# Row norms of an attention-like score matrix: scores with swapped operands, squares on ScalarE, the transpose by VectorE blocks and DMAs

## The chip, the cores and the metric

The kernel runs on one core of a Trainium2 chip. A core has TensorE (matrix products, with weight loads that overlap them), VectorE, ScalarE, GpSimd, and a queue on SyncE that starts most of its DMAs; the engines run side by side and wait for one another through semaphores. The metric is the device time in microseconds (us), from launch to the last result. Before the change it is 2290.54 us, the median of three runs (2290.47 to 2291.78).

## What is computed

The input x holds 128 matrices of 128 rows (nodes) and 512 columns, in float32; adj is one 128x128 matrix. Four layers follow one another, each with a residual and a layer norm over the 512 columns:

```python
# layer 0: x = layernorm(x + (adj @ x) @ W0 + bias0)
# layer 1: x = layernorm(x + L1(x)), the layer that the change touches:
    q = jnp.einsum('bnd,ed->bne', neuron_states, Wq)
    k = jnp.einsum('bnd,ed->bne', neuron_states, Wk)
    v = jnp.einsum('bnd,ed->bne', neuron_states, Wv)
    rel = jnp.einsum('bnd,bmd->bnm', q, k)
    rel = adjacency.T[None, :, :] * rel
    rel = rel / jnp.linalg.norm(rel, axis=2, keepdims=True)
    return jnp.einsum('bnm,bmd->bnd', rel, v)
# layer 2: graph attention (softmax over a masked leaky relu) and elu
# layer 3: relu of a row maximum of adj @ x, plus a bias, added to x
```

In layer 1, rel has a row for each query n and a column for each key m. Its rows are divided by their Euclidean norm, which is a sum over m, and the last product sums over m too.

## The kernel before

The 128 matrices go through in 32 groups of G = 4. Every step of every layer is a small function with a place in time (in slots of about 2.48 us); all of them are sorted by place, so that the layers of neighbouring groups interleave and each engine gets its instructions in that order. Group g's places are 28 slots after those of group g - 1. The names below are the ones that the profile shows; P = 128, K = 4 blocks of the 512 columns, D = 512.

```python
TABLE = dict(
    load=[-20], y=row(0.5, 1), ..., y_w=row(7, 1, 7), ...
    turn=row(21.4, 1), x_sums=row(25.3, 0.5), m=row(28, 1, 7), scores=row(36.5, 1),
    masked=[39.95], norms=[42.5], inverse=[43.1], v=row(42, 1, 7), attend=row(50.6, 1),
    residual=row(51.0, 1), ...
    turn_att=[68.6], with_beta=[69.0], gather=row(71.5, 1), ...
    widen=[98.7, 100.0, 103.6, 104.6], ..., store=[108.5],
)
# the last groups have places of their own (LAST)
```

Layer 1 does not form q and k. It forms xT (x turned, a tile of 512 columns on 4 blocks), then tT, the product of xT with the joined weight m_qk = Wq^T Wk, turned as well. From these two come the scores. Before, they are formed with the key m on the partitions and the query n along the free axis, which is the way round that the last product needs for its stationary operand (a TensorE product sums over partitions: out = lhsT^T rhs):

```python
def scores(b):
    if b == 0:
        s["p"] = bank(f"p_rel_{g}")
    for k in range(K):
        pe.matmul(
            s["p"][:, b * P : (b + 1) * P],
            s["xT"][:, k, b * P : (b + 1) * P],
            s["tT"][:, k, b * P : (b + 1) * P],
            start=(k == 0),
            stop=(k == K - 1),
        )

def masked():
    s["rel"] = work.tile([P, G, P], FP, tag="rel", name=f"rel_{g}", bufs=2)
    dve.tensor_tensor(
        s["rel"], s["p"].rearrange("p (b n) -> p b n", b=G), adj_b, ALU.mult
    )
    s["sq"] = work.tile([P, G, P], FP, tag="sq", name=f"sq_{g}")
    pool.tensor_tensor(s["sq"], s["rel"], s["rel"], ALU.mult)
```

The squared norm of a query is then a sum over partitions. TensorE makes it, as a product of the squares with a column of ones:

```python
def norms():
    p = bank(f"p_n_{g}")
    for b in range(G):
        pe.matmul(p[:, b : b + 1], s["sq"][:, b, :], ones, start=True, stop=True)
    s["p"] = p

def inverse():
    n2 = small.tile([P, G], FP, tag="n2", name=f"n2_{g}")
    dve.tensor_copy(n2, s["p"][:, :G])
    s["rn"] = small.tile([P, G], FP, tag="rn", name=f"rn_{g}")
    pool.tensor_tensor(s["rn"], n2, mhalf, ALU.pow)

def attend(b):
    s["o", b] = bank(f"p_o1_{g}_{b}")
    pe.matmul(s["o", b], s["rel"][:, b, :], s["v"][:, b, :], start=True, stop=True)
```

The division by the norm comes after that product, in the residual on VectorE (x2 = o * rn + x1). The weighted products m, v, y_w and z_w are seven block products each, three PSUM buffers at a time; their results are copied by ScalarE (fresh blocks) or added by VectorE:

```python
ORDER = (1, 2, 6, 5, 7, 3, 4)
REGION = {1: 0, 6: 0, 7: 0, 4: 0, 2: 1, 5: 2, 3: 2}
...
    def out(i):
        p, dst = r[REGION[i]], c(*BLOCK[i])
        if fresh and i in (1, 6, 5, 4):
            act.copy(dst, p)
        else:
            dve.tensor_tensor(dst, p, dst, ALU.add)
```

In the profile r_y, r_m, r_v and r_z are these products, p_rel the scores, p_n the norms, p_o the product with v, p_a, p_z, p_xT, p_eT and p_s products of the other layers.

Of the kernel before, what the change touches and what calls it, by code (L numbers as in the profile page):

```python
# [8 lines left out]
FP = mybir.dt.float32  # L9
AF = mybir.ActivationFunctionType  # L10
# [19 lines left out]
def kernel(  # L30
# [31 lines left out]

    nc = tc.nc
    pe, dve, act, pool = (InOrder(tc, e) for e in (nc.tensor, nc.vector, nc.scalar, nc.gpsimd))
    B, N, D = x.shape
    P = 128
    assert N == P and D % P == 0
    K = D // P
    H = D // 2
    G = 4  # L70
    NG = B // G
# [8 lines left out]
    def bank(name):  # L80
        return psum.tile([P, D], FP, tag="ps", name=name)
# [10 lines left out]
    def load(g):  # L92
        x1[g] = data.tile([P, G, D], FP, tag="x1", name=f"x1_{g}", bufs=3)
        if g == 0:
            for b in range(G):
                nc.sync.dma_start(x1[g][:, b, :], x[b])
        else:
            nc.sync.dma_start(x1[g], x[g * G : (g + 1) * G].rearrange("b n d -> n b d"))

    load(0)  # L100
    w0_sb = const.tile([P, K, D], FP)
# [19 lines left out]

    ident = const.tile([P, P], FP)
    make_identity(nc, ident)
    ones = const.tile([P, 1], FP)
    dve.memset(ones, 1.0)
    mhalf = const.tile([P, G], FP)
    dve.memset(mhalf, -0.5)

# [2 lines left out]
    pe.transpose(pt[:, :P], adj_sb, ident)  # L131
    act.copy(adjT, pt[:, :P])
    adj_b = adj_sb[:, None, :].to_broadcast([P, G, P])

    m_qk = const.tile([P, K, D], FP)
    wvT = const.tile([P, K, D], FP)
# [82 lines left out]
    def emit(at, f, *args):  # L219
        pieces.append((at, lambda: f(*args)))  # L220

    def each(at, f):
        for b in range(len(at)):
            emit(at[b], f, b)

    def row(at, step, n=G):
        return [at + i * step for i in range(n)]
# [3 lines left out]
        load=[-20], y=row(0.5, 1), bias=row(1.3, 1), y_sums=row(5.2, 0.5), y_w=row(7, 1, 7),  # L231
        stats0=row(14.4, 0.4), norm0=[16.2], apply0=row(16.8, 0.33),
        turn=row(21.4, 1), x_sums=row(25.3, 0.5), m=row(28, 1, 7), scores=row(36.5, 1),
        masked=[39.95], norms=[42.5], inverse=[43.1], v=row(42, 1, 7), attend=row(50.6, 1),
        residual=row(51.0, 1), dots=row(54.2, 1.1), norm1=[55.2], scale=[58.8],
        apply1=row(65.4, 0.33),
        spread=[61.6], leaky=[62.0], weighted=[63.4], greatest=[64.3], exps=[64.4],
# [23 lines left out]
        ),  # L261
        NG - 1: dict(
            m=[0.0, 1.73, 3.46, 5.2, 7.4, 9.1, 10.8], scores=row(12.7, 0.9), masked=[16.4],
            norms=[20.2], inverse=[21.1], v=[16.7, 18.4, 21.0, 22.7, 25.3, 27.9, 30.5],
            attend=row(33.2, 0.86), residual=row(34.1, 1.65), norm1=[40.65], dots=row(40.7, 1.53),
            scale=[47.0], apply1=row(47.5, 0.8), spread=[48.9], leaky=[49.4], weighted=[51.0],
            greatest=[52.4], exps=row(53.2, 0.6), divide=row(53.9, 0.6),
# [170 lines left out]
    def layer1(g, t):  # L438
        s = {}

        def turn(b):
            if b == 0:
                s["xT"] = work.tile([P, K, G * P], FP, tag="aT_x", name=f"xT_{g}")
            p = bank(f"p_xT_{g}_{b}")
            for k in range(K):
                pe.transpose(
                    p[:, k * P : (k + 1) * P], x1[g][:, b, k * P : (k + 1) * P], ident
                )
            act.copy(
                s["xT"][:, :, b * P : (b + 1) * P], p.rearrange("p (k n) -> p k n", k=K)  # L450
            )

        def begin_middle():
            s["tT"] = work.tile([P, K, G * P], FP, tag="nat", name=f"tT_{g}", bufs=3)

        def begin_values():
            s["v"] = work.tile([P, G, D], FP, tag="nat", name=f"v_{g}", bufs=3)

        def middle_block(nh, ch):
            return s["tT"][:, 2 * ch : 2 * ch + 2, 2 * P * nh : 2 * P * (nh + 1)]  # L460

# [3 lines that stand above are left out]
            for k in range(K):  # L465
                pe.matmul(
                    s["p"][:, b * P : (b + 1) * P],
                    s["xT"][:, k, b * P : (b + 1) * P],
                    s["tT"][:, k, b * P : (b + 1) * P],
                    start=(k == 0),  # L470
                    stop=(k == K - 1),
                )

        def masked():
            s["rel"] = work.tile([P, G, P], FP, tag="rel", name=f"rel_{g}", bufs=2)
            dve.tensor_tensor(
                s["rel"], s["p"].rearrange("p (b n) -> p b n", b=G), adj_b, ALU.mult
            )
            s["sq"] = work.tile([P, G, P], FP, tag="sq", name=f"sq_{g}")
            pool.tensor_tensor(s["sq"], s["rel"], s["rel"], ALU.mult)  # L480

        def norms():
            p = bank(f"p_n_{g}")
            for b in range(G):
                pe.matmul(p[:, b : b + 1], s["sq"][:, b, :], ones, start=True, stop=True)
            s["p"] = p

        def inverse():
            n2 = small.tile([P, G], FP, tag="n2", name=f"n2_{g}")
            dve.tensor_copy(n2, s["p"][:, :G])  # L490
            s["rn"] = small.tile([P, G], FP, tag="rn", name=f"rn_{g}")
            pool.tensor_tensor(s["rn"], n2, mhalf, ALU.pow)

        def attend(b):
            s["o", b] = bank(f"p_o1_{g}_{b}")
            pe.matmul(s["o", b], s["rel"][:, b, :], s["v"][:, b, :], start=True, stop=True)

        def residual(b):
            if b == 0:
                x2[g] = data.tile([P, G, D], FP, tag="x2", name=f"x2_{g}")  # L500
            dve.scalar_tensor_tensor(
                x2[g][:, b, :],
                s["o", b],
                s["rn"][:, b : b + 1],
                x1[g][:, b, :],
                op0=ALU.mult,
                op1=ALU.add,
            )
            stats(s, f"1_{g}", b, x2[g][:, b, :])


        def dots(b):
            if b == 0:
                s["d"] = small.tile([P, 2, G], FP, tag="d12", name=f"d12_{g}")
            for i in range(2):
                scr = work.tile([P, D], FP, tag="scr", name=f"scr_{g}_{b}_{i}", bufs=2)
                dve.scalar_tensor_tensor(
                    scr,
                    x2[g][:, b, :],
                    1.0,  # L520
                    wa[:, i, :],
                    op0=ALU.mult,
                    op1=ALU.mult,
                    accum_out=s["d"][:, i, b : b + 1],
                )

        def scale_dots():
            for i in range(2):
                dve.scalar_tensor_tensor(
                    s["d"][:, i, :],  # L530
                    s["mv"][:, :, 0],
                    wa_sum[:, i : i + 1],
                    s["d"][:, i, :],
                    op0=ALU.mult,
                    op1=ALU.add,
                )
            dve.tensor_tensor(
                s["d"], s["d"], s["r", 0][:, None, :].to_broadcast([P, 2, G]), ALU.mult
            )
            s12[g] = s["d"]  # L540

        each(t["turn"], turn)
        left_factors(t["x_sums"], s, "xT", "s_x", f"x_{g}", 1)
        product(t["m"], f"m_{g}", by_columns, s, "m", middle_block, True, begin_middle)
        each(t["scores"], scores)
        emit(t["masked"][0], masked)
        emit(t["norms"][0], norms)
        emit(t["inverse"][0], inverse)
        product(t["v"], f"v_{g}", by_rows, s, "v", rows_of(lambda: s["v"]), True, begin_values)
        each(t["attend"], attend)  # L550
        each(t["residual"], residual)
        each(t["dots"], dots)
        emit(t["scale"][0], scale_dots)
        norm(t["norm1"], t["apply1"], s, f"1_{g}", lambda: x2[g])
# [139 lines left out]
    def layer3(g, t):  # L694
        s = {}

        def widen(b):
            s["a", b] = bank(f"p_a_{g}_{b}")
            pe.matmul(s["a", b], adjT, x3[g][:, b, :], start=True, stop=True)

        def top(b):
            x = x3[g][:, b, :]
            mx = small.tile([P, 1], FP, tag="mx", name=f"mx_{g}_{b}")
            dve.tensor_reduce(mx, s["a", b], AX.X, ALU.max)
            tp = small.tile([P, 1], FP, tag="top", name=f"top_{g}_{b}")
            dve.tensor_scalar(tp, mx, b3_sb, 0.0, op0=ALU.add, op1=ALU.max)
            act.activation(x, x, AF.Identity, bias=tp)

        def store(i):
            for b in range(i * n, i * n + n):  # L710
                nc.sync.dma_start(out[g * G + b], x3[g][:, b, :])

        n = G // len(t["store"])
        each(t["widen"], widen)
        each(t["top"], top)
        each(t["stats3"], lambda b: stats(s, f"3_{g}", b, x3[g][:, b, :]))
        norm(t["norm3"], t["apply3"], s, f"3_{g}", lambda: x3[g])
        each(t["store"], store)
# [42 lines left out]
```

## Time and profile before

| engine | busy us | share of the span of 2288.5 us |
|---|---|---|
| TensorE, matrix products | 2250.7 | 98% |
| TensorE, weight loads | 1914.8 | 84% |
| VectorE | 1577.0 | 69% |
| ScalarE | 1005.3 | 44% |
| GpSimd | 959.2 | 42% |

| group of instructions (whole run) | count | mean ns of one |
|---|---|---|
| TensorE p_n<-ones,sq, one column | 256 | 240 |
| TensorE weight load of p_n | 256 | 192 |
| TensorE weight load of p_o | 256 | 191 |
| VectorE rel<-p_rel,adj_sb, 128x512 | 32 | 680 |
| VectorE copy n<-p_n, 128x4 | 32 | 151 |
| VectorE e<-e,rs, 128x128 | 4 | 293 |
| GpSimd sq<-rel, 128x512 | 32 | 1051 |
| ScalarE Exp, 128x128 | 128 | 390 |
| ScalarE read of the accumulator after it | 128 | 187 |
| ScalarE table load | 1 | 1283 |

A product of float32 stands as two records, with a weight load before each. Ends of matmul records are modelled, and neighbours overlap; starts are better to reckon with. The 16 DMA engines are busy a tenth of the time or so after the start; the queue's hardware moved 70.86 MB in 37,536 packets, in 8.7% of 16 engines' span.

### The profile page before, as it was taken

What the parts mean: (1) busy time and instruction counts of PE and PEld (TensorE: products, weight loads), DVE (VectorE), ACT (ScalarE), POOL (GpSimd) and SP (SyncE); (2) the same over time, 40 slices, a digit from 0 to 9 for tenths busy, and PEclk for the clock granted to TensorE, in tenths of its full rate; (3) what the DMA queues carried; (4) which work ended last, traced back from release to release, by engine and by line L of the source; (5) the groups of instructions that cost most, each with busy time, mean ns of one, the idle gap of its engine ahead of it and who ended that gap; (6) DMA issues with size and microseconds to landing.
All of it is one profiled execution on the core that took longest, in us unless ns stands there. A gap on an engine that the chain in (4) does not pass through costs nothing.

```text
span 2288.5 us, 31182 instructions
## 1 busy us (share of the span) xinstructions
PE 2250.7 (98%) x11809; PEld 1914.8 (84%) x11809; DVE 1577.0 (69%) x3319; ACT 1005.3 (44%) x1800; POOL 959.2 (42%) x775
## 2 busy tenths in 40 slices
PE   7999999999999999999999999999999999999996
PEld 5888888888888888888888888888888888888873
DVE  4656776666776667766667766667767677666677
ACT  2224444444444454444444444444444544444435
POOL 4434444344444334444344443444443344443422
PEclk9999999999999999999999999999999999999998
DMA  4000011100111100111100111001111001110001
GB/s 162 19 19 10 28 38 38 37 21 18 38 37 37 38 19 19 38 37 38 37 10 28 38 37 37 21 18 38 37 37 38 19 20 37 37 38 19 9 12 55
DMA packets 38886, 75.21 MB, mean 33 GB/s; under 512 B 3024, under 2 KB 3152, under 8 KB 38736
## 3 DMA queue, kind: packets, MB, share of 16 engines
q1 hardware_dynamic: 37536, 70.86, 8.7%
q10 hardware_dynamic: 1200, 2.36, 0.3%
q8 instruction: 93, 1.52, 0.3%
q14 instruction: 57, 0.47, 0.1%
HBM read 39.65 MB, written 33.55 MB: 32 GB/s over the span
## 4 chain that ended last, share of the span: by engine, by line
PE 94%; DVE 4%; POOL 1%; ACT 1%; issue 1%; DMA 0%; ACTq 0%; DVEq 0%; POOLq 0%
PE r_y L26 17%; PE r_v L26 16%; PE r_m L26 16%; PE r_z L26 16%; PE p_z L26 5%; PE p_rel L26 5%; PE p_o L26 5%; PE p_a L26 5%; PE p_y L26 5%; PE p_xT L26 2%; DVE x L26 1%; PE p_n L26 1%; DVE st L26 1%; PE p_eT L26 1%; PE p_m L26 1%; PE p_s L26 1%
## 5 line engine op out<-in xcount | busy, mean ns | idle before, releaser
L26 ACT ACTIVATE x<-x,nmean,rstd 128x512 f32<-128x512 f32 x512 | 386.4, 809 | 128.0 <-DVE nmean L26 127.9
L26 DVE BATCH_NORM_STATS2 st<-x 128x6 f32<-128x512 f32 x512 | 352.4, 688 | 75.3 <-ACT x L26 66.6
L26 POOL TENSOR_TENSOR rstd<-ve,mhalf 128x4 f32<-128x4 f32 (+1 forms) x134 | 144.5, 1078 | 245.3 <-DVE ve L26 241.3
L26 POOL TENSOR_TENSOR x<-x,bias_sb 128x512 f32<-128x512 f32 x128 | 174.8, 1368 | 145.5 <-PE p_y L26 145.5
L26 DVE SCALAR_TENSOR_TENSOR scr<-x,wa 128x512 f32<-128x512 f32 x256 | 214.9, 891 | 0.0
L26 ACT ACTIVATE x<-x,top 128x512 f32<-128x512 f32 x128 | 92.4, 722 | 254.1 <-DVE top L26 189.7
L26 DVE TENSOR_TENSOR x<-r_y,x 128x512 f32<-128x512 f32 x224 | 152.9, 683 | 54.4 <-PE r_y L26 44.5
L26 DVE TENSOR_TENSOR v<-r_v,v 128x512 f32<-128x512 f32 x96 | 65.8, 685 | 177.0 <-PE r_v L26 174.0
L26 POOL TENSOR_TENSOR s_x<-xT 128x512 f32<-128x512 f32 x64 | 82.2, 1285 | 222.2 <-ACT xT L26 222.2
L26 ACT COPY yT<-p_y 128x512 f32<-128x512 f32 x128 | 75.0, 586 | 206.0 <-PE p_y L26 206.0
L26 DVE SCALAR_TENSOR_TENSOR x<-p_o,rn,x 128x512 f32<-128x512 f32 x128 | 95.9, 749 | 99.5 <-PE p_o L26 96.5
L26 DVE SCALAR_TENSOR_TENSOR x<-m,x 128x512 f32<-128x512 f32 x128 | 115.1, 899 | 61.7 <-ACT m L26 51.3
L26 ACT COPY c<-r_z 128x512 f32<-128x512 f32 x124 | 72.6, 585 | 175.9 <-DVE scr L26 151.5
L26 PEld LDWEIGHTS p_y<-adjT,x 128*128 128x128 f32 x1024 | 135.3, 194 | 12.9 <-ACT adjT L26 5.0
L26 PEld LDWEIGHTS p_z<-eT,x 128*128 128x128 f32 x1024 | 135.4, 194 | 8.3 <-DVE x L26 1.2
L26 PE MATMUL p_y<-adjT,x 128*128 128x128 f32 x1024 | 136.1, 278 | 6.2 <-ACT adjT L26 4.7
L26 PEld LDWEIGHTS p_rel<-tT,xT 128*128 128x128 f32 x1024 | 134.2, 192 | 7.4 <-DVE tT L26 0.8
L26 PE MATMUL p_a<-x,adjT 128*128 128x512 f32 x256 | 133.6, 607 | 3.5 <-DVE mx L26 1.8
L26 PE MATMUL p_z<-eT,x 128*128 128x128 f32 x1024 | 136.4, 277 | 0.4 <-DVE x L26 0.4
L26 PE MATMUL p_rel<-tT,xT 128*128 128x128 f32 x1024 | 135.0, 275 | 0.6 <-DVE tT L26 0.6
L26 POOL TENSOR_TENSOR s_z<-zT 128x512 f32<-128x512 f32 x31 | 39.2, 1265 | 223.9 <-ACT zT L26 223.9
L26 PE MATMUL p_o<-v,rel 128*128 128x512 f32 x256 | 130.6, 594 | 0.0
(120 smaller groups left out, 5075.2 us busy)
## 6 DMA issues: line engine op xcount, KB each, us to landing
out_dram<-x SPq DMA_DIRECT2D x128, 256.0 KB, 2.0
x<-in_x_dram SPq DMA_DIRECT2D x31, 1024.0 KB, 5.2
w_sb<-in_L_gnn_weight_dram ACTq DMA_DIRECT2D x1, 1024.0 KB, 5.7
x<-in_x_dram SPq DMA_DIRECT2D x4, 256.0 KB, 7.5
wq_sb<-in_L_gnn_Wq_dram SPq DMA_DIRECT2D x1, 1024.0 KB, 11.7
wk_sb<-in_L_gnn_Wk_dram SPq DMA_DIRECT2D x1, 1024.0 KB, 14.6
w_sb<-in_L_gnn_W_dram ACTq DMA_DIRECT2D x1, 1024.0 KB, 10.2
wv_sb<-in_L_gnn_Wv_dram SPq DMA_DIRECT2D x1, 1024.0 KB, 13.7
```

Source lines behind the costliest of these rows:

```text
L26: return lambda *args, **kw: self.tc.keep_in_program_order(op(*args, **kw))
```

## The change

The scores are multiplied the other way round, so that the query n lies on the partitions. A row norm is then a sum along the free axis, and ScalarE can form it while it squares, by its accumulator: no product with ones and no copy out of PSUM. The product with v still needs the key m on the partitions, so rel has to be turned. VectorE turns it in blocks of 32x32 within their bands of 32 partitions, and sixteen DMAs per group carry the blocks from band to band, SBUF to SBUF. Two matrices of a pair are interleaved element by element, so that each run of a DMA is 64 elements (256 bytes) long; the product with v then reads its weights with a step of two elements. The purpose is to take the norm products off TensorE. The DMAs on SyncE's queue (loads, these moves, stores) are kept in program order.

```diff
+    sync = InOrder(tc, nc.sync)
+    Q = P // 32
-            nc.sync.dma_start(x1[g], x[g * G : (g + 1) * G].rearrange("b n d -> n b d"))
+            sync.dma_start(x1[g], x[g * G : (g + 1) * G].rearrange("b n d -> n b d"))
...
-    ones = const.tile([P, 1], FP)
-    dve.memset(ones, 1.0)
+    adjT_b = adjT[:, None, :].to_broadcast([P, G, P])
...
-        masked=[39.95], norms=[42.5], inverse=[43.1], v=row(42, 1, 7), attend=row(50.6, 1),
+        masked=[39.95], squares=[40.4], turn_rel=[40.3],
+        move_rel=row(41.2, 0.1), inverse=[42.5], v=row(42, 1, 7), attend=row(50.6, 1),
...  (the last group)
-            norms=[20.2], inverse=[21.1], v=[16.7, 18.4, 21.0, 22.7, 25.3, 27.9, 30.5],
+            squares=[17.2], turn_rel=[17.1], move_rel=row(18.0, 0.1), inverse=[20.0], v=[16.7, 18.4, 21.0, 22.7, 25.3, 27.9, 30.5],
...  (scores)
+                    s["tT"][:, k, b * P : (b + 1) * P],
                     s["xT"][:, k, b * P : (b + 1) * P],
-                    s["tT"][:, k, b * P : (b + 1) * P],
...  (masked)
-                s["rel"], s["p"].rearrange("p (b n) -> p b n", b=G), adj_b, ALU.mult
-            )
-            s["sq"] = work.tile([P, G, P], FP, tag="sq", name=f"sq_{g}")
-            pool.tensor_tensor(s["sq"], s["rel"], s["rel"], ALU.mult)
-
-        def norms():
-            p = bank(f"p_n_{g}")
+                s["rel"], s["p"].rearrange("p (b n) -> p b n", b=G), adjT_b, ALU.mult
+            )
+
+        def squares():
+            s["n2"] = small.tile([P, G], FP, tag="n2", name=f"n2_{g}")
             for b in range(G):
-                pe.matmul(p[:, b : b + 1], s["sq"][:, b, :], ones, start=True, stop=True)
-            s["p"] = p
+                scr = work.tile([P, P], FP, tag="sq", name=f"sq_{g}_{b}", bufs=2)
+                act.activation(
+                    scr, s["rel"][:, b, :], AF.Square, accum_out=s["n2"][:, b : b + 1]
+                )
+
+        def turn_rel():
+            s["relB"] = work.tile([P, 2, Q, 2 * P // Q], FP, tag="relB", name=f"relB_{g}")
+            s["relT"] = work.tile([P, 2, 2 * P], FP, tag="relT", name=f"relT_{g}")
+            for b in range(G):
+                dve.transpose(
+                    s["relB"][:, b // 2].rearrange("p q (u j) -> p q u j", j=2)[:, :, :, b % 2],
+                    s["rel"][:, b, :].rearrange("p (q u) -> p q u", q=Q),
+                )
+
+        def move_rel(a):
+            n = P // Q
+            for q in range(Q):
+                sync.dma_start(
+                    s["relT"][q * n : (q + 1) * n, :, 2 * a * n : 2 * (a + 1) * n],
+                    s["relB"][a * n : (a + 1) * n, :, q, :],
+                )
 
         def inverse():
-            n2 = small.tile([P, G], FP, tag="n2", name=f"n2_{g}")
-            dve.tensor_copy(n2, s["p"][:, :G])
             s["rn"] = small.tile([P, G], FP, tag="rn", name=f"rn_{g}")
-            pool.tensor_tensor(s["rn"], n2, mhalf, ALU.pow)
+            pool.tensor_tensor(s["rn"], s["n2"], mhalf, ALU.pow)
...  (attend)
-            pe.matmul(s["o", b], s["rel"][:, b, :], s["v"][:, b, :], start=True, stop=True)
+            pe.matmul(
+                s["o", b],
+                s["relT"][:, b // 2, :].rearrange("p (n j) -> p n j", j=2)[:, :, b % 2],
+                s["v"][:, b, :],
+                start=True,
+                stop=True,
+            )
...  (store)
-                nc.sync.dma_start(out[g * G + b], x3[g][:, b, :])
+                sync.dma_start(out[g * G + b], x3[g][:, b, :])
```

More of the change, by code (lines that the diff above doesn't have):

```diff
@@ L454, in begin_middle @@
             s["tT"] = work.tile([P, K, G * P], FP, tag="nat", name=f"tT_{g}", bufs=3)
-        def begin_values():
-            s["v"] = work.tile([P, G, D], FP, tag="nat", name=f"v_{g}", bufs=3)
         def middle_block(nh, ch):
@@ L494, in attend, with begin_values @@
+        def begin_values():
+            s["v"] = work.tile([P, G, D], FP, tag="nat", name=f"v_{g}", bufs=3)
         def attend(b):
             s["o", b] = bank(f"p_o1_{g}_{b}")
-            pe.matmul(s["o", b], s["rel"][:, b, :], s["v"][:, b, :], start=True, stop=True)
+            pe.matmul(
[5 more added lines that the diff above has]
+            )
@@ L546, in layer1 @@
         emit(t["masked"][0], masked)
-        emit(t["norms"][0], norms)
+        emit(t["squares"][0], squares)
+        emit(t["turn_rel"][0], turn_rel)
+        each(t["move_rel"], move_rel)
         emit(t["inverse"][0], inverse)
```

## The prediction

> **What bounds the kernel now.** I read the page's first part and its chain, then TensorE's waits, then one period of the trace, and last the groups that the change touches. First part and chain:
>
> ```profile
> PE 2250.7 (98%) x11809; PEld 1914.8 (84%) x11809; DVE 1577.0 (69%) x3319; ACT 1005.3 (44%) x1800; POOL 959.2 (42%) x775
> ...
> PE 94%; DVE 4%; POOL 1%; ACT 1%; issue 1%; DMA 0%; ACTq 0%; DVEq 0%; POOLq 0%
> ```
>
> TensorE is busy 98% of the span and carries 94% of the chain that ended last. Busy matmul rows overlap, so the share alone proves little. The stretches table for one group of four matrices in the steady part settles it:
>
> ```profile
> 1206.00:1275.46 69.46, 69.46 (x370) 59.61 (x369) 48.01 (x103) 31.27 (x56) 29.92 (x25) 1.00 0.09 31
> ```
>
> The columns are the stretch, its length, then the busy time of TensorE, its weight loads, VectorE, ScalarE and GpSimd. TensorE has no gap: the 69.46 us period is its instruction stream laid end to end. The list of TensorE's own waits adds up to about 25 us over the run, and each entry occurs once or twice, at the start or the tail; none recurs by group. So only two things can move the time: a shorter TensorE stream, or a new wait that TensorE sees.
>
> TensorE's timeline around the row norms; columns are start, length, engine, operation, tiles, count:
>
> ```profile
> 1242.57 1.89 PE L26 MATMUL r_v<-wvT,xT 128*128 128x256 f32 x8
> 1244.29 0.95 PE L26 MATMUL p_n<-ones,sq 128*128 128x1 f32 x8
> 1245.10 1.10 PE L26 MATMUL p_a<-x,adjT 128*128 128x512 f32 x2
> 1246.05 1.89 PE L26 MATMUL r_v<-wvT,xT 128*128 128x256 f32 x8
> 1247.77 1.05 PE L26 MATMUL p_z<-eT,x 128*128 128x128 f32 x8
> 1248.66 1.02 PE L26 MATMUL p_a<-x,adjT 128*128 128x512 f32 x2
> 1249.52 1.89 PE L26 MATMUL r_v<-t_v,s_x 128*128 128x256 f32 x8
> ```
>
> The ends of matmuls are modelled and overlap, so I use steps from start to start. From p_n to the next r_v is 1246.05 - 1244.29 = 1.76 us; the p_a within it costs 1249.52 - 1248.66 = 0.86 us where it stands alone. The four norm products therefore take 0.90 us of the period, though each makes one column: their eight weight loads are what is paid.
>
> Next the slack of the other engines at the same place. VectorE, then ScalarE, from the score product's mask on (the last column is idle time before, and its releaser):
>
> ```profile
> 1239.82 0.68 DVE L26 TENSOR_TENSOR rel<-p_rel,adj_sb 128x512 f32<-128x512 f32 x1
> 1240.60 0.69 DVE L26 TENSOR_TENSOR x<-r_y,x 128x512 f32<-128x512 f32 x1
> 1241.21 0.68 DVE L26 TENSOR_TENSOR eT<-p_eT,beta_i 128x512 f32<-128x512 f32 x1
> 1242.77 0.69 DVE L26 TENSOR_TENSOR x<-r_y,x 128x512 f32<-128x512 f32 x1 [0.88 <-PE r_y L26]
> ```
>
> ```profile
> 1239.33 2.93 ACT L26 ACTIVATE x<-x,nmean,rstd 128x512 f32<-128x512 f32 x4 [2.58 <-DVE nmean L26]
> 1244.49 0.59 ACT L26 COPY v<-r_v 128x512 f32<-128x512 f32 x1 [2.23 <-PE r_v L26]
> ```
>
> VectorE has an idle 0.88 us and ScalarE 2.23 us just where the new work goes in. The consumer of the turned matrix comes much later: the first p_o starts at 1266.88 us, 26 us after the mask.
>
> [...] No strided weight load is in this trace.
>
> **The change, part by part.**
>
> 1. Norm products leave TensorE: 32 groups x 0.90 us = -28.8 us, all on the path, since TensorE is never idle there. The last group's step is alike (2203.96 to 2204.87 us).
>
> 2. Scores with the operands swapped: the same 16 products, in 32 records per group of 128 columns over 128x128 weights. The step stays 0.88 to 0.89 us per matrix: 0.
>
> 3. GpSimd loses the squares (32 x 1.05 = 33.6 us), VectorE the copy of n (32 x 0.15 = 4.8 us). Neither engine bounds: 0.
>
> 4. ScalarE gets four Squares with accumulator per group. By the Exp row 390 ns and by the accumulator read 187 ns, 128 x 0.577 = 74 us of busy time; ScalarE goes from 44% to about 48%. The four Exps start every 0.39 us (1230.85, 1231.24, 1231.63, 1232.02), so four Squares fill 1.56 us. They begin when the four applies end, at 1242.26, and end near 1243.9, before the copy of v at 1244.49: hidden, 0. The inverse norms come earlier than before, because n waited for TensorE and VectorE until 1247.10.
>
> 5. VectorE gets four block transposes. [...] p_z wants eT only at 1247.77: 0.
>
> 6. Sixteen DMAs per group move rel between partitions. A store's issue takes 332 ns on the queue (its row) and lands after 2.0 us. 16 x 0.332 + 2.0 = 7.3 us after the transposes, near 1249 us. By bytes: 256 KB in 1024 pieces of 256 B; a packet of before took 8.7% x 16 x 2288.5 / 37,536 = 85 ns of one engine at mostly 2 KB, so at most 64 x 0.085 = 5.4 us on 16 engines. p_o is then due at 1266.0: about 16 us spare. In queue order the load of two groups later stands before them (1207.89, when 1 MB needs 5.2 us) and stores some 26 us after them, so neither is held up. 0.
>
> 7. p_o reads its weights at a step of two. [...]
>
> 8. The last group has less room. There ScalarE's Squares stand before the copy of v that started at 2201.95; they wait for rel until 2202.4, so that copy ends near 2204.6, while the third r_v step, which adds into the same bank, would now start at 2203.96: about +0.6 us. relT is whole near 2203.5 + 7.3 = 2210.8, p_o starts at 2217: 0.
>
> Sum: 2290.5 - 28.8 + 0.6 = 2262.3; with 0.7 us for small tail effects, **2263 us**, -1.2%. The period should go from 69.46 to 68.56 us.
>
> **Rivals.**
>
> A. The transfer becomes the wait. If each DMA had to follow the landing of the one before, 16 x 2.0 = 32 us would be needed where 25 are there: TensorE would stall some 7 us per group, 32 x 7 = 224 us, about 2490. Against it: four DMAs of before were issued within 2.18 us at the start, while each took 7.5 us to land, so they overlap. About 4%.
>
> B. TensorE pays for p_o. Weights at a step of two could load at half rate; the first load of three of the four p_o hides behind a transpose step of only 0.11 us, so it would add 3 x 0.1 us; and the first p_o now waits for many DMA semaphores, perhaps 0.2 us. 32 x 0.5 = 16 us, time 2279. For it: nothing in the trace excludes it. About 15%.
>
> C. VectorE or ScalarE slips into the path. If a transpose takes 0.6 us, the four take 2.4, the last x<-r_y slips by about 1.5 us and the bank that the second r_v needs comes late, by some 0.5 us per group: 2279 again. A table reload for Square between Exps, 1.28 us twice a group, would stay hidden in most groups. About 8%.
>
> D. The norm step's time is not given back, because something else sets the period. Against it: 69.46 of 69.46 us busy. 3%.
>
> **Range and chances.** The gain is capped at 28.8 us = 1.26% as no other TensorE work goes, so faster by over 2% (under 2244.7) needs a surprise: 0.02. Slower by over 2% (above 2336) needs A: 0.05. Within 2%: 0.93. The low end, 2257, allows for the step being a little undersized; the high end, 2279, takes in B and C.
>
> **What would show it.** Right: no p_n row, 11,809 - 256 = 11,553 TensorE records, a period of 68.56 us still gap-free, relT landing some 9 us after the mask, no entry for relT among TensorE's waits, p_o's weight loads at about 190 ns. Wrong: a recurring wait of p_o for a DMA (A), p_o's loads well above 190 ns or steps near them longer (B), r_v waiting for VectorE's x or ScalarE's v in every group (C).

## The result, and the profile after

The changed kernel takes 2262.82 us (median of 4 runs, 2262.06 to 2265.08) against 2291.16 us of the kernel before beside it: a ratio of 0.9878, 95% interval 0.9861 to 0.9895. The prediction was 2263 us.

The first part of the page and the chain of the changed kernel:

```profile
PE 2221.2 (98%) x11553; PEld 1884.2 (83%) x11553; DVE 1599.1 (71%) x3414; ACT 1043.4 (46%) x2056; POOL 924.4 (41%) x743
...
PE 93%; DVE 4%; POOL 1%; ACT 1%; issue 1%; DMA 0%; ACTq 0%; DVEq 0%; POOLq 0%
```

TensorE has 256 matrix records fewer, just the norm products, and still carries nearly the whole chain. VectorE and ScalarE have more to do, GpSimd less. One period of the steady part, from one start of r_y to the next (length, then busy time of TensorE, weight loads, VectorE, ScalarE, GpSimd):

```profile
1143.84:1212.43 68.59, 68.59 (x361) 58.72 (x360) 48.96 (x106) 32.45 (x64) 28.85 (x24) 1.00 0.11 36
```

It is still without a gap, and 69.46 - 68.59 = 0.87 us shorter; every period from the fourth group on has this length. TensorE's timeline at the place of the norm products, and at the first p_o:

```profile
1228.53 1.89 PE L26 MATMUL r_v<-wvT,xT 128*128 128x256 f32 x8
1230.26 1.02 PE L26 MATMUL p_a<-x,adjT 128*128 128x512 f32 x2
1231.11 1.89 PE L26 MATMUL r_v<-wvT,xT 128*128 128x256 f32 x8
...
1251.95 1.03 PE L26 MATMUL p_o<-v,relT 128*128 128x512 f32 x2
1252.82 1.89 PE L26 MATMUL r_z<-t,s_z 128*128 128x256 f32 x8
```

Between the two r_v there is p_a alone, in 0.85 us where 1.76 us were. p_o follows without a wait. The rows of what was added, from the views of the tiles rel, relB and relT (minimum, median and maximum in ns):

```profile
L26 ACT ACTIVATE sq<-rel x128: 292/293/310, 77.4 to 2177.0; 128x128 f32<-128x128 f32 x128
L26 DVE STREAM_TRANSPOSE relB<-rel x128: 269/273/316, 77.4 to 2176.8; 128x128 f32<-128x128 f32 x128
L26 SPq DMA_DIRECT2D relT<-relB x512: 585/595/1882, 78.3 to 2186.7; - x171
L26 PEld LDWEIGHTS p_o<-v,relT x256: 193/197/197, 94.9 to 2194.7; 128*128 128x128 f32 x128
```

Sixteen issues of such moves fill 10.18 us of SyncE's queue per group, and a move lands 1.8 us after its issue.

### The profile page after: what moved, and what is told of

It is laid out like the page before. It is cut to its first block, busy times and chain, and to the rows that moved or that the text cites. A ratio compares the mean times of both kernels' runs of the same rounds, so it can differ in the third digit from the quotient of the medians.

```text
span 2260.3 us, 31788 instructions
## 1 busy us (share of the span) xinstructions
PE 2221.2 (98%) x11553; PEld 1884.2 (83%) x11553; DVE 1599.1 (71%) x3414; ACT 1043.4 (46%) x2056; POOL 924.4 (41%) x743
## 4 chain that ended last, share of the span: by engine, by line
PE 93%; DVE 4%; POOL 1%; ACT 1%; issue 1%; DMA 0%; ACTq 0%; DVEq 0%; POOLq 0%
PE r_y L26 17%; PE r_v L26 16%; PE r_m L26 16%; PE r_z L26 16%; PE p_rel L26 5%; PE p_z L26 5%; PE p_o L26 5%; PE p_y L26 5%; PE p_a L26 5%; PE p_xT L26 2%; DVE x L26 1%; DVE st L26 1%; PE p_eT L26 1%; PE p_m L26 1%; PE p_s L26 1%
## 5 line engine op out<-in xcount | busy, mean ns | idle before, releaser
L26 PEld LDWEIGHTS p_rel<-xT,tT 128*128 128x128 f32 x1024 | 134.1, 191 | 7.4 <-DVE tT L26 0.8
L26 PE MATMUL p_rel<-xT,tT 128*128 128x128 f32 x1024 | 134.9, 275 | 0.6 <-DVE tT L26 0.6
L26 PE MATMUL p_z<-eT,x 128*128 128x128 f32 x1024 | 134.8, 275 | 0.4 <-DVE x L26 0.4
L26 ACT COPY tT<-r_m 128x512 f32<-128x512 f32 x128 | 75.7, 591 | 123.7 <-PE r_m L26 123.7
```

What stands on the lines that cost most here:

```text
L26: return lambda *args, **kw: self.tc.keep_in_program_order(op(*args, **kw))
```

## The experiments

Two theories stood against each other. **H**: the whole gain is TensorE's step of 0.90 us per group, and all that the change adds is hidden in slack. **R**: part of the gain comes from elsewhere (GpSimd relieved, a PSUM buffer free), or the additions cost something that a larger gain covers. All times below are medians beside runs of the kernel before on the same chip.

### The norm products left out of the kernel before

Their sum is left out: the inverse norm is taken of a constant 1, so the rows are not normalised.

```diff
-        emit(t["norms"][0], norms)
-            dve.tensor_copy(n2, s["p"][:, :G])
-            pool.tensor_tensor(s["rn"], n2, mhalf, ALU.pow)
+            pool.tensor_tensor(s["rn"], one, mhalf, ALU.pow)      # one: a tile of 1.0
```

> The kernel before with the norm products left out (the inverse norm is taken of a constant 1, so the rows are not normalised) and the VectorE copy of their result with them; scores, squares on GpSimd and everything else as before. Theory H (the whole gain is TensorE's 0.90 us step per group, and all that the change adds is hidden): 2291.2 - 32 x 0.90 = 2262, period 68.56 us, and within 2 us of the changed kernel. Theory R (the change gains in part elsewhere, by the relief of GpSimd or of a PSUM bank, or the products were worth more and the additions cost some of it): a time clearly off 2262; 2270 or more if the relief elsewhere counts, 2250 or less if the additions cost 12 us or more.

Measured: 2261.8 us, ratio 0.9877 (0.9860 to 0.9893), period 68.57 us, from one start of r_y to the next:

```profile
1143.42 3.62 PE L26 MATMUL r_y<-w_sb,yT 128*128 128x256 f32 x16
1211.99 3.62 PE L26 MATMUL r_y<-w_sb,yT 128*128 128x256 f32 x16
```

This kernel has none of the additions, and GpSimd still makes its squares; it is 1.0 us faster than the change. So the additions together cost about 1 us, which is within the spread of the runs: H.

### The norm products put back into the changed kernel

```diff
+        def norms():
+            p = bank(f"p_n_{g}")
+            for b in range(G):
+                pe.matmul(p[:, b : b + 1], s["rel"][:, b, :], ones, start=True, stop=True)
+            n2 = small.tile([P, G], FP, tag="nn", name=f"nn_{g}")
+            dve.tensor_copy(n2, p[:, :G])
```

> The changed kernel with the four one-column products per group put back as extra work at their old place (of rel with a column of ones, copied by VectorE, the result unused). H: 2262.8 + 32 x 0.90 = 2291.6, the time of before within 2 us, period about 69.5 us. R: less than that, 2275 to 2285, if part of the gain came from elsewhere.

Measured: 2290.77 us, ratio 0.9999 (0.9990 to 1.0007), the time of before, and a period of 69.48 us. TensorE's timeline of this kernel:

```profile
1243.34 1.89 PE L26 MATMUL r_v<-wvT,xT 128*128 128x256 f32 x8
1245.06 0.95 PE L26 MATMUL p_n<-ones,rel 128*128 128x1 f32 x8
1245.87 1.10 PE L26 MATMUL p_a<-x,adjT 128*128 128x512 f32 x2
1246.82 1.89 PE L26 MATMUL r_v<-wvT,xT 128*128 128x256 f32 x8
```

From p_n to r_v it is again 1.76 us, although GpSimd's squares are gone and the scores are swapped. R falls from both sides: leaving the products out gives the gain without the change, and putting them back takes it away with the change in place. The products and their PSUM buffer go and come together in both kernels; that the buffer is not what counts rests on the periods, which have no gap with or without it.

### The moves twice, and three times

The same moves go ahead of the real ones once or twice more, into a tile that nobody reads.

```diff
+            if a == 0:
+                for i in range(1):                     # range(2) for three times
+                    x = work.tile([P, 2, 2 * P], FP, tag="relX", name=f"relX_{g}_{i}")
+                    for c in range(Q):
+                        for q in range(Q):
+                            sync.dma_start(
+                                x[q * n : (q + 1) * n, :, 2 * c * n : 2 * (c + 1) * n],
+                                s["relB"][c * n : (c + 1) * n, :, q, :],
+                            )
```

> The changed kernel with sixteen more moves per group, into a tile that nobody reads, queued ahead of the real ones. By the trace of the changed kernel, issues 0.595 us apart and 1.8 us to landing: 32 x 0.595 + 1.8 = 20.8 us from 1227.5, so relT is whole near 1248.3 and p_o starts at 1251.95. H: hidden in 31 groups, in the last about 6 us late (2177.1 + 20.8 = 2197.9 against 2191.9): 2269. Rival (the moves already touch TensorE, by contention or waits): tens of us more, 2290 or above.

Measured: 2279.37 us, 16.6 us more than the change. TensorE's waits in it:

```profile
PE p_o L26 <- DMA relT<-relB: 12.6, 2, 6.8
```

The columns are the total, the number of times and the longest. Thirty groups hide nearly ten more microseconds of moves (16 x 0.595); two do not. The last one is late by 6.8 us, as expected, and the first by 5.8 us, which the expectation forgot: at the start p_o stands nearer to the mask, as no other group's work lies between. The remaining 4 us are mostly slower products just after the two waits (the last p_o x8 takes 5.99 instead of 3.82 us), on which more below.

> Thirty-two more moves per group ahead of the real ones: 48 x 0.595 + 1.8 = 30.4 us against 24.5 us from the first issue to p_o, so p_o waits some 5.9 us per group. H with the slack read from the trace: 2262.8 + 31 x 5.9 + 14.5 = about 2460, with a recurring wait of p_o for a DMA. Rival (the slack is larger than read, as issues overlap more): 2265 to 2300.

Measured: 2662.27 us. The wait recurs, so the moves do reach a limit, but its cost was put too low. TensorE's waits, then its timeline and the stretches around one wait (the third figure from the end is the granted clock):

```profile
PE p_o L26 <- DMA relT<-relB: 321.4, 32, 18.3
```

```profile
1152.61 2.05 PE L26 MATMUL p_o<-v,relT 128*128 128x512 f32 x2 [9.72 <-DMA relT<-relB]
1154.45 3.43 PE L26 MATMUL r_z<-t,s_z 128*128 128x256 f32 x8
```

```profile
1152.60:1158.00 5.40, 5.39 (x13) 3.67 (x14) 1.63 (x3) 0.00 (x0) 0.00 (x0) 0.54 0.22 85
1158.00:1170.00 12.00, 12.00 (x55) 9.51 (x54) 9.04 (x19) 4.14 (x7) 5.95 (x5) 1.00 0.37 129
```

p_o waits 9.7 us per group where 5.9 were expected: the 32 extra issues took 22.8 instead of 19.0 us, partly because the queue waited for its own earlier moves into the reused tile (33.8 us in 45 waits). Waits make 321 of the 399 us. The other 78 us, 2.4 us per group, are the clock: after the wait it is granted at 0.54 for 5.4 us (0.46 x 5.4 = 2.5 us), and r_z takes 3.43 instead of 1.89 us. A wait of TensorE thus cost a quarter more than its length here.

### The weights of p_o at a step of one

Here relB and relT hold the four matrices one after another; the moves have runs of 128 bytes, twice as many.

```diff
-                s["relT"][:, b // 2, :].rearrange("p (n j) -> p n j", j=2)[:, :, b % 2],
+                s["relT"][:, b, :],
```

> The changed kernel without the interleaving of pairs: relB and relT hold the four matrices one after another, p_o reads its weights at a step of one, and each move writes runs of 32 elements (128 bytes), twice as many. If the step of two costs what the trace shows (weight loads 197 instead of 191 ns, p_o's step 0.87 instead of 0.86 us): 32 x 4 x 0.01 = 1.3 us less, 2261.5, with loads at 191 ns. If the 6 ns are the operand's place and not its step: 2262.8 and loads still at 197 ns. If the runs of 128 bytes made the moves longer than the slack (over 24 us): 2280 or more; expected is an issue of 0.6 to 0.7 us, hidden.

Measured: 2262.51 us, ratio 0.9880 (0.9867 to 0.9894). The rows of the moves and of the loads:

```profile
L26 SPq DMA_DIRECT2D relT<-relB x512: 585/599/1581, 78.3 to 2186.2; - x171
L26 PEld LDWEIGHTS p_o<-v,relT x256: 186/190/192, 94.8 to 2194.1; 128*128 128x128 f32 x128
```

The loads are back at a median of 190 ns, and the period is 68.57 instead of 68.59 us; both agree with a cost of the step of two of some 0.02 us per group, 0.6 us in all. The total can't confirm that, as its runs spread over 3 us. An issue took 599 ns in place of 595, so twice as many runs made no difference to it: the interleaving of pairs bought nothing that these runs show.

### More transposes on VectorE

```diff
+            x = work.tile([P, G, Q, P // Q], FP, tag="relX", name=f"relX_{g}")
+            for i in range(12):
+                dve.transpose(
+                    x[:, i % G], s["rel"][:, i % G, :].rearrange("p (q u) -> p q u", q=Q)
+                )
```

> Twelve more block transposes per group on VectorE, into a tile that nobody reads, ahead of the four: 12 x 0.205 = 2.5 us more at the place where VectorE has little idle left (0.17 us behind the change). If VectorE is close to the path there: the last x<-r_y slips by about 2.4 us, from 1228.73 to about 1231.1, its bank comes free near 1231.8, the second r_v (due at 1231.11) waits about 0.7 us in each group, 2262.8 + 32 x 0.7 = 2285. If other idle time takes it up: 2263 to 2266.

Measured: 2276.75 us, 13.9 us above the change, and a period of 68.97 us. So 2.4 us more on VectorE at this place put 0.4 us per group on the path. But not by the way that the expectation named: the second r_v starts with no wait. ScalarE carries the delay. Its timeline in this kernel, and TensorE's:

```profile
1244.48 0.72 ACT L26 ACTIVATE x<-x,top 128x512 f32<-128x512 f32 x1 [2.72 <-DVE top L26]
...
1248.64 0.59 ACT L26 COPY v<-r_v 128x512 f32<-128x512 f32 x1
```

```profile
1248.12 1.05 PE L26 MATMUL p_z<-eT,x 128*128 128x128 f32 x8
1249.29 1.99 PE L26 MATMUL r_v<-wvT,s_x 128*128 128x256 f32 x8
```

VectorE's maximum (top) is late, ScalarE waits for it in order, and the copy of v behind it ends at 1249.23, just ahead of an r_v that could have started 0.28 us sooner (1248.12 + 0.89). Behind the change itself, the same copy ends 0.9 us before that r_v wants it (1241.55 against 1242.45). That is the slack left there. The other 0.1 us of the longer period is in the late r_v itself: 1.83 us from its start to the next (1251.12), where that step takes 1.73 in the changed kernel (1242.45 to 1244.18).

### The same device for x

If TensorE's stream is all that counts, its 16 transposes of x per group (p_xT, 4 x 0.44 us) can go the same way: four VectorE transposes of 128x512 and sixteen moves replace them and ScalarE's copies. They stand three to five slots earlier than the transposes they replace, and rel has one buffer in place of two.

```diff
-            p = bank(f"p_xT_{g}_{b}")
-            for k in range(K):
-                pe.transpose(
-                    p[:, k * P : (k + 1) * P], x1[g][:, b, k * P : (k + 1) * P], ident
-                )
-            act.copy(
-                s["xT"][:, :, b * P : (b + 1) * P], p.rearrange("p (k n) -> p k n", k=K)
-            )
+            dve.transpose(
+                s["xB"][:, :, b, :].rearrange("p k (q u) -> p k q u", q=Q),
+                x1[g][:, b, :].rearrange("p (k q u) -> p k q u", k=K, q=Q),
+            )
+        def move_x(a):      # for every q: band a of xB to band q of xT, runs of 32 elements
```

> The changed kernel with the same device used once more: x is no longer turned by TensorE (16 transposes per group into PSUM, copied out by ScalarE) but by four VectorE transposes of 128x512 and sixteen DMAs with runs of 128 bytes, placed as soon as layer 0 is normed. TensorE loses 4 x 0.44 = 1.75 us per group. H (TensorE's stream is all that counts, additions are hidden while they fit their slack): 2262.8 - 32 x 1.75 = 2207, period 66.8 us. Rival (the moves, 16 x 0.6 + 2 = 11.6 us and perhaps 5 to 10 more with four times the runs, or VectorE, come too late for the sums that GpSimd makes of xT some 12 us after): r_m or r_v wait for xT in each group, 2240 to 2400.

Measured: 2273.85 us, slower than the change. TensorE's waits, and GpSimd and VectorE at the same time:

```profile
PE r_m L26 <- DMA xT<-xB: 28.6, 2, 19.4
PE r_y L26 <- DVE x L26: 9.1, 30, 0.9
```

```profile
1212.80 1.72 POOL L26 TENSOR_TENSOR s_x<-xT 128x512 f32<-128x512 f32 x1
1214.47 1.72 POOL L26 TENSOR_TENSOR s_x<-xT,s_x 128x512 f32<-128x512 f32 x1
...
1217.66 3.18 POOL L26 TENSOR_TENSOR x<-x,bias_sb 128x512 f32<-128x512 f32 x2
```

```profile
1213.32 1.75 DVE L26 SCALAR_TENSOR_TENSOR scr<-x,wa 128x512 f32<-128x512 f32 x1
...
1217.97 1.75 DVE L26 SCALAR_TENSOR_TENSOR scr<-x,wa 128x512 f32<-128x512 f32 x1
```

Two things went wrong. At the start nothing hides the moves, 28.6 us in the first two groups. Later, the sums that GpSimd makes of xT come late, and so do the additions of the bias that follow them on GpSimd. About half of VectorE's dot products now fall beside one or the other, where it was a quarter in the changed kernel: those take up to 1.75 us instead of 0.68, GpSimd's sums 1.72 instead of 1.27, and VectorE makes r_y wait, 9.1 us in 30 times. Not everything on VectorE was longer there: c<-r_z,c at 1214.99, with r_z in PSUM, took 0.68 us beside the sum at 1214.47. Why the dot products and the sums take longer side by side was not shown. TensorE's waits for the moves and for VectorE (28.6, 9.1 and, at r_m for tT, 7.8 us) make 45.5 us of the 71 by which the profiled run (2278.36 us) missed 2207; how the rest divides stays open.

Two versions take this apart. The first turns x on TensorE in groups 0 and 1:

```diff
+    FIRST = {0: dict(turn=row(21.4, 1)), 1: dict(turn=row(21.4, 1), ...)}
+            if g < 2:            # pe.transpose and act.copy as in the changed kernel
```

> As the kernel that also turns x by VectorE and DMAs, but groups 0 and 1 turn x on TensorE as the changed kernel does, since there the products r_m waited 28.6 us for the moves. Its steady period, from start to start of r_v, was 67.74 us against 68.57 of the changed kernel. If the loss lay at the start alone: 2262.8 - 30 x 0.83 = 2238. If the waits only move to group 2: 2250 to 2265.

Measured: 2252.61 us, ratio 0.9836 (0.9821 to 0.9850): 21 us less, not 36. The estimate rested on one period of 67.74 us. In this kernel's trace some take 67.75 us, others 68.11, 69.30 or 69.40: besides r_y, r_m waits for VectorE's tT, 8.3 us in six times. VectorE's lateness costs more than the one period showed. The time lies in the range that was given for waits that only move to group 2, but that is not what happened: no r_m waits for a move any more.

The second gives xT two buffers besides, so that its moves need not wait for r_v of the group before:

```diff
-                s["xT"] = work.tile([P, K, G * P], FP, tag="aT_x", name=f"xT_{g}")
+                s["xT"] = work.tile([P, K, G * P], FP, tag="aT_x", name=f"xT_{g}", bufs=2)
-            s["tT"] = work.tile([P, K, G * P], FP, tag="nat", name=f"tT_{g}", bufs=3)
+            s["tT"] = work.tile([P, K, G * P], FP, tag="nat", name=f"tT_{g}", bufs=2)     # v, c and the loaded weights too
```

> As the one before it, with two buffers for xT, so that the moves need not wait until r_v has read the last of the group before (SyncE's queue waited 3.8 us per group for that), paid for by two instead of three buffers for tT, v and c. The moves then end about 4 us earlier, GpSimd's sums of xT too, and VectorE's dot products, of which four in eight took 1.75 instead of 0.68 us beside those sums, no longer run beside them. If this overlap is what keeps the period above 66.8 us: 2262.8 - 30 x 1.75 = 2210. If VectorE stays behind for another reason: 2230 to 2240, as the kernel before it.

Measured: 2211.16 us (2210.59 to 2211.80), ratio 0.9654 (0.9638 to 0.9670). It leaves nothing out and is faster than both kernels. One period:

```profile
1118.62:1185.43 66.81, 66.81 (x345) 57.15 (x344) 51.76 (x110) 30.36 (x60) 28.93 (x24) 1.00 0.21 52
```

It is gap-free again and 1.78 us shorter than the change's, the 4 x 0.44 us of p_xT. VectorE's dot products with one buffer and with two (in the last three figures: busy time in us, mean ns of one, idle time before):

```profile
L26 DVE SCALAR_TENSOR_TENSOR scr<-x,wa 128x512 f32<-128x512 f32 x256 | 293.7, 1198 | 0.0
L26 DVE SCALAR_TENSOR_TENSOR scr<-x,wa 128x512 f32<-128x512 f32 x256 | 199.9, 833 | 0.0
```

Of the 30 waits of r_y for VectorE none is left in the list of TensorE's waits.

## Why the prediction was right, step by step

**Step 1, the norm products**, is the source of the gain: 1.76 us from p_n to r_v, less 0.86 for the p_a between them, before and again where the products were put back, and 29.7 us (2291.45 to 2261.8) when they and their copy are taken out of the kernel before. Its size, 28.8 us, was a little too large. "TensorE is never idle there" does not hold in the first group, where a later r_v gives the 0.9 us back as a wait for ScalarE's copy of v:

```profile
90.53 1.99 PE L26 MATMUL r_v<-wvT,s_x 128*128 128x256 f32 x8 [0.91 <-ACT v L26]
```

With the products left out of the kernel before, the same r_v waits 0.91 us too. So the changed kernel gains 0.87 us in each of 30 groups, not 0.90 in 32; the last group is step 8. **Step 2**, swapped scores: the period shows no change from them.

**Steps 3 to 5** were hidden as said. A Square took 293 ns, not the 390 of an Exp, and no table load came with the Squares: the run has one, of 1283 ns, as before. The Squares stand before the last of the four applies, not behind it, and the copy of v still waits 1.07 us for its r_v. For the block transposes the sum has 0, a term that no run of the kernel before shows; in the changed kernel one took 273 ns, some 0.21 us from start to start, and the four 0.90 us (0.89 in the last group). VectorE's idle time before the last x<-r_y fell from 0.88 to 0.17 us, so the slack there was nearly used up.

**Step 6** had its mechanism right and a term too small: an issue of a move takes 595 ns, not a store's 332, so that relT is whole after 16 x 0.595 + 1.8 = 11.3 us instead of 7.3. Of the 24 us there, half is left; twice the moves still hide in all groups but the first and the last. The 5.4 us by bytes took the work to be spread over all 16 engines, which no view shows; a move landed 1.8 us after its issue.

**Step 7**, weights at a step of two, adds nothing to the sum, and no run of the kernel before shows such a load. It was nearly right: the loads took 197 against 191 ns, and p_o's step 0.87 against 0.86 us. Rival B named this at 0.3 us per group; it is 0.02 to 0.03.

**Step 8**, the last group: the copy of v did come late behind the Squares, but r_v waited only 0.15 us for it. The group lost another 0.46 us at p_a, which waited for ScalarE's x. From p_rel to p_o it took 21.56 us after and 21.39 before, so it gave back its whole gain of 0.9 us and 0.2 us more, where 0.6 us were predicted.

The sum is close to the difference of the two profiled spans (2288.5 and 2260.3, 28.2 us apart), but one term in it is not the change's. From the first common r_y (64.26 and 64.28 us) to the last (2129.47 and 2104.06) the gain is 25.4 us; 0.7 us follow up to p_o; and 1.6 us come in the tail between p_o and the products c, where the kernel before ran at a granted clock of 0.69 in that profile and the changed one at 1.00:

```profile
2243.50:2249.00 5.50, 4.79 (x22) 4.33 (x23) 2.57 (x12) 1.96 (x7) 0.00 (x0) 0.69 0.00 0
2217.50:2222.00 4.50, 3.88 (x24) 3.04 (x25) 3.17 (x12) 2.32 (x7) 0.00 (x0) 1.00 0.02 4
```

Half a microsecond more comes after them. The kernel with the products put back took 28.7 us from p_o to c, as the changed one did, where the kernel before took 30.3, so the products are not what lowered the clock there. (TensorE's p_z records sum to 134.8 us in those two and to 136.4 in the kernel before.) The change's own share is thus some 26.6 of the 28.2 us, and the match to 0.2 us is in part luck; the period, predicted 68.56 and measured 68.59, is the better test.

## What to carry to other kernels

When one engine's stream has no gap, count its steps from start to start, and price a change by the steps that it takes out; everything else is checked against the slack at its place, in the first and the last group too; and a kernel with the step left out is a cheap bound on what any rewrite of it can bring. The four one-column products took 0.90 us of the stream, as much as p_z's four of 128 columns (0.89), and the eight weight loads of either stood end to end over 1.08 us; so a row sum was cheaper on an engine that has slack and can accumulate along its free axis. When work moves off the bound engine, look next at what its new timing falls beside: here an extra buffer, which let the moves of x start some 3 us earlier, decided between 2253 and 2211 us.

## What the runs showed of the hardware that was not expected

- A DMA from SBUF to SBUF over 32 partitions took 595 ns to issue with 64 runs of 256 bytes and 599 ns with 128 runs of 128 bytes; a store of 128 rows of 2 KB took 332 ns.
- After TensorE had waited 9.7 us, its clock was granted at 0.54 over the next 5.4 us, and each such wait cost 2.4 us on top.
- VectorE's dot products of x and wa, both in SBUF, took up to 1.75 us beside GpSimd's sums and additions instead of 0.68, and the sums 1.72 instead of 1.27 us.
